# Sums of 40 rows turned round in a graph network's edge stage: features on partitions, W3 applied at once, counts from the activation, narrower tables, two banks

## The chip, the cores and the metric

The kernel runs on one core of a Trainium2 chip. The metric is the device time of one execution in microseconds (us). The data are one graph of 12,500 nodes with 48 features and 400,000 edges, all in fp32 on the path that matters here.

## The reference

Two layers, each fed with h = relu(layernorm(x)) and added to x. The edges are sorted by target (`dst`).

```python
def L0(x, src, dst, W, b):                    # first layer
    deg = bincount(src);  s = where(deg > 0, deg ** -0.5, 0)
    msg = (s[src] * s[dst])[:, None] * x[dst]
    return relu(segment_sum(msg, src, n) @ W.T + b)

def L1(x, src, dst, edge_attr, W1, b1, W2, b2, W3, b3):   # second layer
    edge = concatenate([x[src], x[dst], edge_attr], -1)   # 48 + 48 + 16 = 112
    h = relu(edge @ W1 + b1)                              # 128 features
    h = relu(h @ W2 + b2)                                 # 128 features
    message = h @ W3 + b3                                 # 48 features
    cnt = segment_sum(1, dst, n)
    return x + segment_sum(message, dst, n) / maximum(cnt, 1)[:, None]

h = relu(layernorm(x));  x = x + L0(h, src, dst, ...)
h = relu(layernorm(x));  x = x + L1(h, src, dst, edge_attr, ...)
```

The change touches the second layer's sums over the edges of a target, W3 and the counts. Since W3 is linear, both kernels sum h (128 features) over the edges of a target first and multiply the sums by W3; b3 enters times the count. The kernels also hold max(h@W2, -b2) instead of relu(h@W2 + b2), and add b2 back by way of `cb`, which is b2@W3 + b3, times the count.

## The kernel before

The stages ahead (to 2025.9 us) sort out the windows, count degrees, run the first layer, and leave in DRAM `htab`, the 48 features of every node, and `btab`, the part of W1 that belongs to the target, applied to every node (`x[dst] @ W1[48:96]`, 128 wide). With the zeros of `zero` the two tables `utab` of sums are cleared near the start, by 14 DMAs on SP's queue (helper `clear`).

The edge stage ("e1") goes over 782 chunks of 4 x 128 = 512 edges (the last chunk is one tile of 128). Two chunks (`Q`) share a window: 40 neighbouring target rows (`W`), in which all their edges end. For each chunk there are five steps:

- `fetch`: ACT copies 16 edge features into the tile `et` (L997); POOL issues four gathers of 128 rows each from `htab` into it (the helper `gather`, L225); ACT makes from the targets the one-hot window `mv[64:104]`, 40 rows by 512 edges, with a Square and a Relu (helper `window_of`, L641 and L647): relu(1 - (target - row)^2). Every second chunk SP loads the 40 rows of `btab` under the weights of W1, into one of five tiles `wk` (L994).
- `turn`: four transposes on PE (L1009) and a copy by ACT (L1010) put the 64 features of the 512 edges into `mv[:64]`.
- `first`: one matmul of 104 rows, that is W1 on the features and the window's rows of `btab` through the one-hot (L1015), and ACT's Relu with b1 (L1019).
- `second`: four matmuls with h1 as weights, so that edges lie on partitions (L1026); DVE makes the one-hot `oh` of each edge's place in the window (L1031), writes 1.0 into the 129th column of h2 (L1039), and takes the maximum with -b2 (L1040).
- `summed`: four matmuls with `oh` as weights (40 columns) and h2 as moving side (129 columns) into `u_all`, which holds 40 rows (L1053). A window's eight matmuls accumulate. At the second chunk ACT takes the 40x129 sums out (L1062) and SP writes them into one of the two tables `utab` at the window's first row (L1063); windows in turn use one half and the other of `u_all`, and one table and the other.

fp32 matmuls run in two passes (the transposes in one), so the profile counts eight for four matmuls and two for `first`. In the loop, iteration c issues `fetch(c)`, then `summed(c-6)`, `second(c-4)`, `first(c-2)` and `turn(c)`, 782 + 6 iterations in all. The order on each engine is fixed by a scheduler when the kernel is compiled: on PE it is in each iteration the sums of c-6, h2 of c-4, h1 of c-2 and the transposes of c. The number of buffers limits how far an engine runs ahead: `et` has 8, `mv` 6, `h1`, `oh` and `h2` 4 each; in PSUM `et_ps`, `h1_ps` and `h2_ps` have 2 banks each and `u_all` and `m_ps` one each.

```python
u_all = ps.tile([W, 2, 256], FP, name="u_all", bufs=1)      # L1067: two halves of one bank
...
for step, late in ((summed, 6), (second, 4), (first, 2), (turn, 0)):
    if 0 <= c - late < NC1:
        step(run[c - late])
```

When all windows of a block of nodes are written, `finish` (a generator of which each iteration runs one step) loads that block of both tables (L1078), adds them (L1085), copies the counts out of column 128 (L1088), transposes the sums on PE (L1094), takes them out (L1097), applies W3 (L1101), adds the counts times `cb` (L1106, L1112) and hands over to `updated`, which divides by the counts, adds the residuals (L955 to L960) and stores. There are nine blocks: six of 14 x 128 nodes, then 8, 4 and 2 x 128.

Of the kernel before, what the change touches and what calls it, by code (L numbers as in the profile page):

```python
# [20 lines left out]
def kernel(  # L21
# [36 lines left out]
    nc = tc.nc  # L58
    N, F = x.shape
    E = src.shape[0]  # L60
    EF = edge_attr.shape[1]
    H = w2.shape[0]
# [3 lines left out]
    ROWS = NH * P  # L66
# [3 lines left out]
    TABLE = ROWS + P  # L70
    B = 4
    F1 = F + 1
    H1 = H + 1
    W = 40
    Q = 2
    NCH = NT // B
# [2 lines left out]
    NC1 = NCH + 1  # L79
# [23 lines left out]
    blocks, h0 = [], 0  # L103
# [102 lines left out]
    ltab = dram.tile([ND, RUN + P], FP, name="ltab")  # L206
    dltab = dram.tile([NS, ND, P], BF, name="dltab")
    acc1 = dram.tile([TABLE, F1], FP, name="acc1")
    utab = [dram.tile([ROWS, H1], FP, name=f"utab_{k}") for k in range(2)]
    ZH = 14  # L210

    def clear(tables, w, engines, pool):
# [138 lines left out]
    clear(utab, H1, (nc.sync, nc.sync), rp)  # L351


    w0_t = const.tile([F, F], FP, name="w0_t")
# [40 lines left out]
    k = 2  # L395
# [240 lines left out]
    def window_of(db, p0, c, to):  # L636


        a = c % VG * B * P
        n = B if c < NCH else TAIL  # L640
        nc.scalar.activation(  # L641
            to.rearrange("p (j i) -> p j i", j=n),
            db[p0 : p0 + W, a : a + n * P].rearrange("p (i j) -> p j i", j=n),
            AF.Square,
            bias=wid[p0 : p0 + W, c // Q : c // Q + 1],
        )
        nc.scalar.activation(to, to, AF.Relu, scale=-1.0, bias=unit[p0 : p0 + W])  # L647
        return n

    hview = htab.rearrange("(h p) f -> p h f", p=P)  # L650
# [318 lines left out]
    with tc.If(fast > 0) as branch:  # L969
        with tc.tile_pool(name="e1", bufs=3) as wp, tc.tile_pool(  # L970
# [9 lines left out]
            def fetch(c):  # L980
                n = B if c < NCH else TAIL
                if c % VG == 0:
                    group["db"] = targets(wp, 64, c)
                    v = min(VG, NCH - c)
                    ea = wp.tile([P, VG, B, EF], FP, name="ea", bufs=2)
                    nc.scalar.dma_start(ea[:, :v], ea_view[:, c : c + v])
                    group["ea"] = ea
                db, ea = group["db"], group["ea"]
                if c == NCH:
                    nc.scalar.dma_start(ea[:, c % VG, 0, :], edge_attr[E4:])  # L990
                if c % Q == 0:
# [10 lines left out]
                window_of(db, 64, c, mv[64:, : n * P])  # L1002
                return dict(c=c, n=n, at=at, wc=wc, et=et, mv=mv)

            def turn(k):
# [16 lines left out]
            def second(k):  # L1022
                n, h1 = k["n"], k["h1"]
                h2_ps = ps.tile([P, B, H], FP, name="h2_ps")
                for j in range(n):
                    nc.tensor.matmul(  # L1026
                        h2_ps[:, j, :], h1[:, j * P : (j + 1) * P], w2_sb, start=True, stop=True
                    )
                c = k["c"]
                oh = wp.tile([P, B, W], FP, name="oh", bufs=4)  # L1030
                nc.vector.tensor_tensor(  # L1031
                    oh[:, :n],
                    rel[:, c * B : c * B + n].unsqueeze(2).to_broadcast([P, n, W]),
                    iota_f[:, None, :W].to_broadcast([P, n, W]),
                    OP.is_equal,
                )
                k["oh"] = oh
                h2 = wp.tile([P, B, H1], FP, name="h2", bufs=4)
                nc.vector.memset(h2[:, :, H:], 1.0)  # L1039
                nc.vector.tensor_tensor(  # L1040
                    h2[:, :n, :H],
                    h2_ps[:, :n],
                    b2_neg[:, None, :].to_broadcast([P, n, H]),
                    OP.max,
                )
                k["h2"] = h2

            def summed(k):
                n, oh, h2 = k["n"], k["oh"], k["h2"]
                q = k["c"] % Q  # L1050
                u_ps = u_all[:, k["c"] // Q % 2, :H1]
                for j in range(n):
                    nc.tensor.matmul(  # L1053
                        u_ps,
                        oh[:, j, :],
                        h2[:, j, :],
                        start=(q == 0 and j == 0),
                        stop=(q == Q - 1 and j == n - 1),
                    )
                if q == Q - 1:  # L1060
                    u = wp.tile([W, H1], FP, name="u", bufs=4)
                    nc.scalar.activation(u, u_ps, AF.Copy)  # L1062
                    nc.sync.dma_start(utab[k["c"] // Q % 2][bass.ds(k["at"], W), :], u)  # L1063

            u_all = ps.tile([W, 2, 256], FP, name="u_all", bufs=1)
            cb_ps = ps.tile([P, B, H], FP, name="m_ps", bufs=1)
            nc.tensor.matmul(  # L1067
                cb_ps[:, 0, :F], b2_col.to_broadcast([H, P]), w3_sb, start=True, stop=True
            )
            cb = wp.tile([P, F], FP, name="cb", bufs=1)  # L1070
            nc.vector.tensor_tensor(cb, cb_ps[:, 0, :F], b3_sb, OP.add)
            HB = blocks[0][1]

            def finish(h0, n):

                us = [wp.tile([P, HB, H1], FP, name=f"uk{k}", bufs=1) for k in range(2)]
# [10 lines left out]
                cnt = wp.tile([P, HB], FP, name="cnt", bufs=1)  # L1087
                nc.vector.tensor_copy(cnt[:, :n], us[0][:, :n, H])  # L1088
                upd = wp.tile([P, HB, F], FP, name="upd", bufs=1)
                for a in range(0, n, B):  # L1090
                    k = min(B, n - a)
                    m_ps = ps.tile([P, B, H], FP, name="m_ps", bufs=1)
                    for j in range(k):
                        nc.tensor.transpose(m_ps[:, j, :], us[0][:, a + j, :H], ident)  # L1094
                    yield
                    u_t = wp.tile([H, B, P], FP, name="u_t", bufs=1)
                    nc.scalar.activation(u_t[:, :k], m_ps[:, :k], AF.Copy)  # L1097
                    yield
                    m_ps = ps.tile([P, B, H], FP, name="m_ps", bufs=1)
                    for j in range(k):  # L1100
                        nc.tensor.matmul(  # L1101
                            m_ps[:, j, :F], u_t[:, j, :], w3_sb, start=True, stop=True
                        )
                    yield
                    cw = wp.tile([P, B, F], FP, name="cw", bufs=1)
                    nc.vector.tensor_tensor(  # L1106
                        cw[:, :k],
                        cnt[:, a : a + k].unsqueeze(2).to_broadcast([P, k, F]),
                        cb[:, None, :].to_broadcast([P, k, F]),
                        OP.mult,  # L1110
                    )
                    nc.vector.tensor_tensor(  # L1112
                        upd[:, a : a + k, :], m_ps[:, :k, :F], cw[:, :k], OP.add
                    )
                    yield
                updated(wp, h0, n, cnt[:, :n], upd[:, :n])

            def go_on():
                if ends and next(ends[0], "end") == "end":
# [1 line left out]

            coming, ends = list(blocks), []
            group, run = {}, []
            for c in range(NC1 + 6):
                run.append(fetch(c) if c < NC1 else None)
                for step, late in ((summed, 6), (second, 4), (first, 2), (turn, 0)):
                    if 0 <= c - late < NC1:
                        step(run[c - late])
                done = c + 1 - 6
                while coming and done >= coming[0][2]:  # L1130
                    h0, n, _ = coming.pop(0)
                    ends.append(finish(h0, n))
                go_on()
# [71 lines left out]
```

## Time and profile before

| | |
|---|---|
| Median of three runs | 6740.73 us (6739.53 to 6771.3) |
| The profiled execution, its own time | 6743.89 us |
| Its span (first to last instruction) | 6742.1 us |
| Mean granted clock of TensorE | 0.860 |
| First gather of the edge stage | 2025.9 us |
| Busy share of the span, PE / ACT / DVE / POOL | 68 / 58 / 38 / 46% |

The profile page lists one execution. In its slices, each column is a fortieth of the span (168.6 us) and a digit the busy share in tenths; the granted clock is in tenths of full speed. In its groups, a row is line, engine, operation, tiles (out <- in), shapes and count, then busy us in all and the mean ns of one, then the idle time of the engine just before these instructions and what ended most of it. In the waits, a row is who waited, for which row's end, us in total, times and the longest. "remote" is an end of a wait which the profile cannot lay to a row; "issue" is time in which the engine waited for nothing that is seen. In the timeline, a row is start us, duration us, engine, line, operation, shapes and count, and in brackets the idle time ahead of it. Releasers are inferred from the order in time, so an engine that finished just before is sometimes named where another had been the cause.

### The profile page before, as it was taken

To read this page: it belongs to the slowest core of one execution; us is meant where nothing else is said; L and a number is where in the kernel's file an instruction comes from. 1 tells how busy PE (TensorE), PEld (TensorE's weight loads), DVE (VectorE), ACT (ScalarE), POOL (GpSimd) and SP (SyncE) were. 2 spreads that over 40 slices of the span, in tenths; PEclk is the share of its full clock that TensorE was granted. 3 is DMA by queue.
4 is the path that set the end of the run, shared out by engine and by line. 5 is a ranking of instruction groups with operands and counts; after the bars stand their busy time and mean duration, and the time that the engine had idled before them with its cause. 6 is when DMAs were issued, how large, how long until landed. Compare 5 with 4: busy or idle time off the path is not lost. (4 is left out here: it accounts for less than half of the span.)

```text
span 6742.1 us, 97110 instructions
## 1 busy us (share of the span) xinstructions
PE 4613.8 (68%) x35368; PEld 3546.1 (53%) x35368; DVE 2539.2 (38%) x4116; ACT 3879.8 (58%) x7051; POOL 3080.8 (46%) x3239
## 2 busy tenths in 40 slices
PE   0400589999994776776777677777676777677777
PEld 0300489999993444544455455445454454445545
DVE  2995799999981111111111111111111111111112
ACT  1600178888884555655556555555555555555555
POOL 0003200000006666666666666666666666666664
PEclk9999699999996888888888888878888887888888
DMA  3001154444432222222222222222222222222221
GB/s 129 14 0 28 35 158 147 148 148 147 145 123 47 40 41 39 52 41 41 39 52 41 41 39 52 40 41 40 53 43 38 41 50 43 39 41 50 43 45 30
DMA packets 397378, 407.60 MB, mean 60 GB/s; under 512 B 227689, under 2 KB 351229, under 8 KB 392382
## 3 DMA queue, kind: packets, MB, share of 16 engines
q1 hardware_dynamic: 168166, 280.50, 14.8%
q0 software_dynamic: 103488, 85.03, 8.5%
q10 hardware_dynamic: 125238, 35.77, 2.3%
q8 instruction: 283, 4.64, 0.3%
q14 instruction: 203, 1.66, 0.1%
HBM read 363.00 MB, written 38.02 MB: 59 GB/s over the span
## 5 line engine op out<-in xcount | busy, mean ns | idle before, releaser
L225 POOL DMA_INDIRECT et<-htab,src_i x3125 | 2964.5, 949 | 3004.1 <-PE m_ps L1067 1300.9
L1053 PE MATMUL u_all<-h,oh 128*40 128x129 f32 x6250 | 1022.4, 314 | 1106.3 <-ACT u L1062 662.3
L1053 PEld LDWEIGHTS u_all<-h,oh 128*40 128x40 f32 x6250 | 739.1, 132 | 1358.3 <-ACT u L1062 773.1
L1019 ACT ACTIVATE h<-h_ps,b_sb 128x512 f32<-128x512 f32 x782 | 534.3, 683 | 1388.5 <-remote 701.4
L1040 DVE TENSOR_TENSOR h<-h_ps,b_neg 128x512 f32<-128x512 f32 x782 | 538.5, 689 | 1765.8 <-PE et_ps L1009 547.9
L1026 PE MATMUL h_ps<-w_sb,h 128*128 128x128 f32 x6250 | 1128.4, 332 | 75.1 <-issue 56.5
L1026 PEld LDWEIGHTS h_ps<-w_sb,h 128*128 128x128 f32 x6250 | 947.9, 231 | 267.2 <-issue 237.1
L842 ACT ACTIVATE rows<-at_ps 128x432 bf16<-128x432 f32 x1830 | 951.2, 531 | 147.9 <-DVE g L801 35.2
L1031 DVE TENSOR_TENSOR oh<-rel,iota_f 128x160 f32<-128x160 f32 x782 | 253.5, 324 | 2063.4 <-remote 679.5
L854 PE MATMUL sum<-rows,ohs 128*128 128x144 bf16 x10976 | 1008.5, 228 | 20.6 <-ACT rows L842 17.4
L1015 PE MATMUL h_ps<-mv,wk 104*128 104x512 f32 x1564 | 936.1, 681 | 28.5 <-issue 28.1
L641 ACT ACTIVATE mv<-db,wid 40x512 f32<-40x512 int32 x782 | 943.2, 1206 | 17.4
L854 PEld LDWEIGHTS <-ohs 128*128 128x128 bf16 x10976 | 855.4, 144 | 26.0 <-issue 19.8
L826 DVE TENSOR_TENSOR ohs<-lo_b,iota_x 128x4096 bf16<-128x4096 bf16 (+1 forms) x350 | 786.1, 2247 | 51.3 <-PE sum L854 33.0
L1009 PEld LDWEIGHTS et_ps<-ident,et 128*64 128x64 f32 x3125 | 365.8, 118 | 727.0 <-issue 618.4
L838 PE MATMUL at_ps<-g,oht 112*128 112x144 bf16 x5488 | 651.1, 226 | 36.0 <-DVE oht L822 35.6
L1009 PE MATMUL et_ps<-ident,et 128*64 128x128 f32 x3125 | 541.6, 286 | 172.1 <-issue 132.1
L647 ACT ACTIVATE mv<-mv,unit 40x512 f32<-40x512 f32 x782 | 560.1, 716 | 19.9
L1010 ACT ACTIVATE mv<-et_ps 64x512 f32<-64x512 f32 x782 | 453.4, 580 | 202.1 <-remote 102.1
L838 PEld LDWEIGHTS <-oht 112*128 112x128 bf16 x5488 | 416.1, 98 | 39.0 <-issue 36.0
L1015 PEld LDWEIGHTS h_ps<-mv,wk 104*128 104x128 f32 x1564 | 286.4, 226 | 43.6 <-issue 43.5
L1062 ACT ACTIVATE u<-u_all 40x129 f32<-40x129 f32 x391 | 106.0, 271 | 316.5 <-remote 215.6
(202 smaller groups left out, 2193.3 us busy)
## 6 DMA issues: line engine op xcount, KB each, us to landing
at<-dltab SPq DMA_DIRECT2D x343, 448.0 KB
db<-in_dst_dram SPq DMA_DIRECT2D x97, 640.0 KB
et<-htab,src_i POOLq DMA_INDIRECT x3125
ea<-in_edge_attr_dram ACTq DMA_DIRECT2D x97, 256.0 KB
utab<-zero SPq DMA_DIRECT2D x14, 903.0 KB
uk<-utab SPq DMA_DIRECT2D x12, 903.0 KB
utab<-u SPq DMA_DIRECT2D x391, 20.2 KB
wk<-btab SPq DMA_DIRECT2D x391, 20.0 KB
```

What stands on the lines that cost most here:

```text
L225: nc.gpsimd.indirect_dma_start(out=into, out_offset=None, in_=table, in_offset=bass.IndirectOffsetOnAxis(ap=idx, axis=0),)
L641: nc.scalar.activation(to.rearrange("p (j i) -> p j i", j=n), db[p0 : p0 + W, a : a + n * P].rearrange("p (i j) -> p j i", j=n), AF.Square ...
L647: nc.scalar.activation(to, to, AF.Relu, scale=-1.0, bias=unit[p0 : p0 + W])
L826: nc.vector.tensor_tensor(ohs[:, :n], lo_b[:, h0 : h0 + n, None, c : c + CG].to_broadcast([P, n, S, CG]), iota_x[:, None].to_broadcast([P, ...
L838: nc.tensor.matmul(ps3[:, i, :], oht[:, k, c % CG, :], g3[:, c, :], start=True, stop=True)
L842: nc.scalar.activation(rows[:, : len(tiles)], ps3[:, : len(tiles)], AF.Copy)
L854: nc.tensor.matmul(sums[k][:, j, :], ohs[:, k, j * P : (j + 1) * P, c % CG], rows[:, i, :], start=(c == 0 and j == 0), stop=(c == ND - 1 a ...
L1009: nc.tensor.transpose(et_ps[:, j * P : (j + 1) * P], et[:, j, :], ident)
L1015: nc.tensor.matmul(h1_ps[:, : n * P], k["wc"], k["mv"][:, : n * P], start=True, stop=True)
L1026: nc.tensor.matmul(h2_ps[:, j, :], h1[:, j * P : (j + 1) * P], w2_sb, start=True, stop=True)
L1040: nc.vector.tensor_tensor(h2[:, :n, :H], h2_ps[:, :n], b2_neg[:, None, :].to_broadcast([P, n, H]), OP.max,)
L1053: nc.tensor.matmul(u_ps, oh[:, j, :], h2[:, j, :], start=(q == 0 and j == 0), stop=(q == Q - 1 and j == n - 1),)
```

## The change

- `summed`: h2 is now the weights and `oh` the moving side, so that the sums come out with 128 features on partitions and 40 rows as columns. They have their own PSUM tile `u_ps`, a whole bank, two of them in turn. ACT takes the 128x40 sums out at the second chunk (L1065, tile `u_t`). In h2 the column of ones goes, and its memset.
- `applied`, a new step eight iterations after `fetch`: one matmul with `u_t` as weights applies W3 (L1072) and writes 40x48 into another part of the same bank (columns 256 to 303, partitions 64 to 103); ACT takes it out (L1074), DVE adds the counts of the two chunks as the 49th column (L1075), SP writes 40x49 into the table (L1078).
- The counts come from the sum that ACT's Relu in `window_of` now writes out (`accum_out`), one number per row of the window and chunk, in the tile `cnt_w`.
- The tables have 49 columns instead of 129, and so have their clears and the loads of `finish`, which loses the transposes, their evictions, W3 and the copy of the counts.
- The loop runs 782 + 8 iterations, and a block is finished two iterations later.

```diff
-    utab = [dram.tile([ROWS, H1], FP, name=f"utab_{k}") for k in range(2)]
+    utab = [dram.tile([ROWS, F1], FP, name=f"utab_{k}") for k in range(2)]
...
-        nc.scalar.activation(to, to, AF.Relu, scale=-1.0, bias=unit[p0 : p0 + W])
+        nc.scalar.activation(
+            to, to, AF.Relu, scale=-1.0, bias=unit[p0 : p0 + W], accum_out=count
+        )
...
-                h2 = wp.tile([P, B, H1], FP, name="h2", bufs=4)
-                nc.vector.memset(h2[:, :, H:], 1.0)
+                h2 = wp.tile([P, B, H], FP, name="h2", bufs=4)
...
             def summed(k):
                 n, oh, h2 = k["n"], k["oh"], k["h2"]
                 q = k["c"] % Q
-                u_ps = u_all[:, k["c"] // Q % 2, :H1]
+                if q == 0:
+                    group["u_ps"] = ps.tile([H, 512], FP, name="u_ps")
+                k["u_ps"] = group["u_ps"]
+                u_ps = k["u_ps"][:, :W]
                 for j in range(n):
                     nc.tensor.matmul(
                         u_ps,
+                        h2[:, j, :],
                         oh[:, j, :],
-                        h2[:, j, :],
                         start=(q == 0 and j == 0),
                         stop=(q == Q - 1 and j == n - 1),
                     )
                 if q == Q - 1:
-                    u = wp.tile([W, H1], FP, name="u", bufs=4)
-                    nc.scalar.activation(u, u_ps, AF.Copy)
-                    nc.sync.dma_start(utab[k["c"] // Q % 2][bass.ds(k["at"], W), :], u)
-
-            u_all = ps.tile([W, 2, 256], FP, name="u_all", bufs=1)
...
+                    u_t = wp.tile([H, W], FP, name="u_t", bufs=3)
+                    nc.scalar.activation(u_t, u_ps, AF.Copy)
+                    k["u_t"] = u_t
+
+            def applied(k):
+                c = k["c"]
+                if c % Q == Q - 1:
+                    m_ps = k["u_ps"][64:K1, 256 : 256 + F]
+                    nc.tensor.matmul(m_ps, k["u_t"], w3_sb, start=True, stop=True)
+                    u = wp.tile([P, F1], FP, name="u", bufs=4)
+                    nc.scalar.activation(u[64:K1, :F], m_ps, AF.Copy)
+                    nc.vector.tensor_tensor(
+                        u[64:K1, F:], cnt_w[64:K1, c - 1 : c], cnt_w[64:K1, c : c + 1], OP.add
+                    )
+                    nc.sync.dma_start(utab[c // Q % 2][bass.ds(k["at"], W), :], u[64:K1, :])
...
             def finish(h0, n):
...
-                for a in range(0, n, B):
-                    z = slice(a, min(a + B, n))
-                    nc.vector.tensor_tensor(us[0][:, z], us[0][:, z], us[1][:, z], OP.add)
-                    yield
...
-                        nc.tensor.transpose(m_ps[:, j, :], us[0][:, a + j, :H], ident)
...
-                            m_ps[:, j, :F], u_t[:, j, :], w3_sb, start=True, stop=True
...
+                u, cnt = us[0][:, :n, :F], us[0][:, :n, F]
+                nc.vector.tensor_tensor(us[0][:, :n], us[0][:, :n], us[1][:, :n], OP.add)
+                yield
+                cw = wp.tile([P, HB, F], FP, name="cw", bufs=1)
...
+                nc.vector.tensor_tensor(cw[:, :n], cw[:, :n], u, OP.add)
...
-            for c in range(NC1 + 6):
+            for c in range(NC1 + 8):
                 run.append(fetch(c) if c < NC1 else None)
-                for step, late in ((summed, 6), (second, 4), (first, 2), (turn, 0)):
+                for step, late in (
+                    (applied, 8), (summed, 6), (second, 4), (first, 2), (turn, 0)
+                ):
...
-                done = c + 1 - 6
+                done = c + 1 - 8
```

In the compiled order of after, PE's work of an iteration is no longer in four clean pieces: transposes stand between the sums, h2 and h1, and L1072 of one window stands between the sums of the next window's two chunks. ACT's L998 (the former L997) stands two chunks ahead of the transposes instead of seven, and L640 (the former L641) one instead of three to four. POOL's order is as before.

More of the change, by code (lines that the diff above doesn't have):

```diff
@@ L72 @@
     F1 = F + 1
-    H1 = H + 1
     W = 40
@@ L349 @@
             nc.scalar.activation(ov[:, c], tp.rearrange("p b q -> p q b"), AF.Copy)
-    clear(utab, H1, (nc.sync, nc.sync), rp)
+    clear(utab, F1, (nc.sync, nc.sync), rp)
     w0_t = const.tile([F, F], FP, name="w0_t")
@@ L634, in window_at, with window_of @@
         return nc.sync.value_load(db[p0 : p0 + 1, a : a + 1], min_val=0, max_val=N - 1)
-    def window_of(db, p0, c, to):
+    def window_of(db, p0, c, to, count):
         a = c % VG * B * P
@@ L1001, in fetch @@
                 mv = wp.tile([K1, B * P], FP, name="mv", bufs=6)
-                window_of(db, 64, c, mv[64:, : n * P])
+                window_of(db, 64, c, mv[64:, : n * P], cnt_w[64:K1, c : c + 1])
                 return dict(c=c, n=n, at=at, wc=wc, et=et, mv=mv)
@@ L1037, in second @@
                 k["oh"] = oh
-                h2 = wp.tile([P, B, H1], FP, name="h2", bufs=4)
-                nc.vector.memset(h2[:, :, H:], 1.0)
+                h2 = wp.tile([P, B, H], FP, name="h2", bufs=4)
                 nc.vector.tensor_tensor(
-                    h2[:, :n, :H],
+                    h2[:, :n],
                     h2_ps[:, :n],
@@ L1060, in summed @@
                 if q == Q - 1:
-                    u = wp.tile([W, H1], FP, name="u", bufs=4)
-                    nc.scalar.activation(u, u_ps, AF.Copy)
-                    nc.sync.dma_start(utab[k["c"] // Q % 2][bass.ds(k["at"], W), :], u)
-            u_all = ps.tile([W, 2, 256], FP, name="u_all", bufs=1)
[L1066 to L1069, printed above, removed]
+                    u_t = wp.tile([H, W], FP, name="u_t", bufs=3)
[12 more added lines that the diff above has]
+                    nc.sync.dma_start(utab[c // Q % 2][bass.ds(k["at"], W), :], u[64:K1, :])
+            cnt_w = wp.tile([P, NC1], FP, name="cnt_w", bufs=1)
+            cb_ps = ps.tile([H, 512], FP, name="u_ps")[:, :F]
+            nc.tensor.matmul(cb_ps, b2_col.to_broadcast([H, P]), w3_sb, start=True, stop=True)
             cb = wp.tile([P, F], FP, name="cb", bufs=1)
-            nc.vector.tensor_tensor(cb, cb_ps[:, 0, :F], b3_sb, OP.add)
+            nc.vector.tensor_tensor(cb, cb_ps, b3_sb, OP.add)
             HB = blocks[0][1]
             def finish(h0, n):
-                us = [wp.tile([P, HB, H1], FP, name=f"uk{k}", bufs=1) for k in range(2)]
+                us = [wp.tile([P, HB, F1], FP, name=f"uk{k}", bufs=1) for k in range(2)]
                 for k in range(2):
@@ L1082, in finish @@
                 yield
-                for a in range(0, n, B):
-                    z = slice(a, min(a + B, n))
-                    nc.vector.tensor_tensor(us[0][:, z], us[0][:, z], us[1][:, z], OP.add)
-                    yield
[L1087 to L1093, printed above, removed]
-                        nc.tensor.transpose(m_ps[:, j, :], us[0][:, a + j, :H], ident)
[L1095 to L1101, printed above, removed]
-                            m_ps[:, j, :F], u_t[:, j, :], w3_sb, start=True, stop=True
[L1103 to L1115, printed above, removed]
@@ L1116, in finish @@
-                updated(wp, h0, n, cnt[:, :n], upd[:, :n])
+                u, cnt = us[0][:, :n, :F], us[0][:, :n, F]
+                nc.vector.tensor_tensor(us[0][:, :n], us[0][:, :n], us[1][:, :n], OP.add)
+                yield
+                cw = wp.tile([P, HB, F], FP, name="cw", bufs=1)
+                nc.vector.tensor_tensor(
+                    cw[:, :n],
+                    cnt.unsqueeze(2).to_broadcast([P, n, F]),
+                    cb[:, None, :].to_broadcast([P, n, F]),
+                    OP.mult,
+                )
@@ L1118, in go_on @@
+                yield
+                nc.vector.tensor_tensor(cw[:, :n], cw[:, :n], u, OP.add)
+                yield
+                updated(wp, h0, n, cnt, cw[:, :n])
             def go_on():
```

## The prediction

> **What bounds the kernel now.** The profiled execution took 6743.89 us, 3.2 us over the median of 6740.73 us of the three runs; its span is 6742.1 us. All sums below are made in this span, and 3 us are taken off at the end. I read the slices first, then the groups, the waits and the timeline.
>
> The slices, POOL's row and the granted clock (each column is 168.6 us):
>
> ```profile
> POOL 0003200000006666666666666666666666666664
> PEclk9999699999996888888888888878888887888888
> ```
>
> From the 13th slice on POOL works without change: it is the edge stage, which runs from the first gather at 2025.9 us to 6742.1 us, 4716 us or 70% of the span. Nearly all that the change touches is here. 782 chunks in 4667 us (2025.9 to the last gather at 6692.7) are 5.97 us a chunk. The groups give the two ends of this:
>
> ```profile
> L225 POOL DMA_INDIRECT et<-htab,src_i x3125 | 2964.5, 949 | 3004.1 <-PE m_ps L1067 1300.9
> L1053 PE MATMUL u_all<-h,oh 128*40 128x129 f32 x6250 | 1022.4, 314 | 1106.3 <-ACT u L1062 662.3
> L1019 ACT ACTIVATE h<-h_ps,b_sb 128x512 f32<-128x512 f32 x782 | 534.3, 683 | 1388.5 <-remote 701.4
> ```
>
> A gather is 0.95 us busy and, back to back, starts 1.25 us after the one before (timeline below). So four gathers are 5.0 us a chunk: POOL's floor for the stage is 3125 x 1.25 = 3906 us. The 750 us between 3906 and 4667 us are pauses of POOL. PE waits 1106 us at one place, the first matmul of the sums (L1053). The waits from 2100 to 6700 us:
>
> ```profile
> PEld u_all L1053 <- ACT u L1062: 773.1, 185, 12.8
> ACT h L1019 <- remote: 692.2, 105, 28.1
> PE u_all L1053 <- ACT u L1062: 662.3, 172, 7.6
> POOL et L225 <- ACT h L1019: 439.7, 143, 4.0
> ACT u L1062 <- remote: 215.6, 55, 7.9
> ```
>
> (PEld and PE are the same wait seen twice.) PE waits for ACT's eviction L1062, since both halves of `u_all` are one tile in one bank; ACT itself waits "remote". The timeline shows what that means:
>
> ```profile
> 3190.39 0.91 PE L1009 MATMUL et_ps<-ident,et 128*64 128x128 f32 x4
> ...
> 3192.59 0.94 POOL L225 DMA_INDIRECT et<-htab,src_i  x1 [0.30 <-issue]
> 3193.07 0.69 DVE L1040 TENSOR_TENSOR h<-h_ps,b_neg 128x512 f32<-128x512 f32 x1 [6.06 <-remote]
> 3195.16 0.69 ACT L1019 ACTIVATE h<-h_ps,b_sb 128x512 f32<-128x512 f32 x1 [6.74 <-remote]
> ...
> 3196.68 0.94 POOL L225 DMA_INDIRECT et<-htab,src_i  x1 [3.15 <-ACT mv L1010]
> ...
> 3197.81 0.27 ACT L1062 ACTIVATE u<-u_all 40x129 f32<-40x129 f32 x1
> ...
> 3198.14 1.94 PE L1053 MATMUL u_all<-h,oh 128*40 128x129 f32 x8 [6.83 <-ACT u L1062]
> ```
>
> PE has done its transposes by about 3191.3 us and stands for 6.83 us. ACT is idle for 6.74 us of that, though the matmuls that L1019 reads had ended at 3190.6; it goes on only when POOL's row of twelve gathers (from 3178.8, the last at 3192.59) has ended. Most such rows (202 of 291) are of exactly twelve, three chunks, then POOL pauses 2.9 us: 15 + 2.9 = 17.9 us for three chunks, the 5.97 us. So POOL runs until it has no buffer, the others learn late of what PE has done, and PE stands at L1053. When the gathers are over (after 6693 us) there is no such wait, and from one L1053 row to the next are 3.39 us (6709.05 to 6712.44).
>
> **The change part by part.**
>
> *The sums.* h2 becomes the weights (128 columns) and the one-hot rows the moving side (40 instead of 129 columns); eight matmul passes a chunk as before. The nearest rows stand side by side near the end, at full clock:
>
> ```profile
> 6724.54 0.99 PE L1101 MATMUL m_ps<-w_sb,u_t 128*128 128x48 f32 x8
> 6725.46 1.08 PE L1053 MATMUL u_all<-h,oh 128*40 128x129 f32 x8
> 6726.47 1.16 PE L1026 MATMUL h_ps<-w_sb,h 128*128 128x128 f32 x8
> ```
>
> Eight passes of the old form take 6726.47 - 6725.46 = 1.01 us; eight with 128 weight columns and 48 moving ones 0.92 us. So the new form is worth between 0 and 0.09 x 782 = -70 us; I take 0, as PE has 1106 us of waits here.
>
> The Trainium skill speaks against this part: "TensorE: Matmul & The Clock Gate", step-by-step section, says that the time of a weight load goes by its columns, with columns / 1.2 ns: an estimate of 107 ns against 33. By this page, if the load were bare, 6250 passes would cost 458 us more. The rows above differ: 128 columns and 40 go at one pace, and the measurement decides.
>
> *W3 at once.* 391 times two passes (L1072): 782 x 0.115 (the L1101 row) = +90 us of PE. The finish loses 98 transposes and 98 matmuls of two passes: 294 x 0.12 = -35 us. Net +55 us at full clock, up to +110 at half; I charge 30, because PE has waits to hide most of it, and keep 0 to 110. The compiled order puts L1072 of a group between the sums of the next group's two chunks; there it waits for the eviction L1065, issued an iteration before. If this eviction is as late as ACT's in the timeline, then all that PE has queued behind it (sums, h2, h1, transposes, hence POOL's buffers) is late with it; that is part of rival D.
>
> *Two banks.* In before the first sum of a group waits for L1062 of the group just finished, about half an iteration earlier in PE's order. In after it waits for L1074 of the group two back, and L1072 for L1065: one to one and a half iterations. So PE gains about one chunk of lead; a wait of 6.8 us is not longer than that lead plus an iteration at half clock (6.2 to 7 us in the trace). What is late next is the pair of banks of `et_ps` and `h1_ps`, whose lead is two iterations, and POOL's buffers.
>
> *ACT.* The Relu of the window gets an accumulator read. The row for it, and its pace:
>
> ```profile
> 94.45 0.23 ACT L364 ACTIVATE spare<-xt 128x48 f32<-128x48 f32 x1
> 94.58 0.19 ACT L364 ACTIVATION_READ_ACCUMULATOR spare<-xt 128x1 f32 x1
> 94.68 0.23 ACT L364 ACTIVATE spare<-xt 128x48 f32<-128x48 f32 x1
> ```
>
> It adds 0.10 (by pace) to 0.19 us. Per pair, one eviction of 0.27 (L1062) gives way to two, 0.25 (L1065, by L997's 0.256) and 0.23 (L1074, by L364): +0.21, or 0.105 a chunk. So +0.205 to +0.295 us a chunk on 3.58 us (L641 1.21, L647 0.72, L1019 0.68, L1010 0.58, L997 0.26, half of 0.27): +160 to +231 us of ACT. As long as the period is 5.97 us a chunk, ACT has over 2 us of idle time in it and the cost is 0; if ACT's idle time cannot be used, all of it counts (rival D). L641 and L998 also come later in ACT's order than before (one and two chunks ahead of the transposes instead of three and seven), which takes cover from ACT.
>
> *DVE.* 782 memsets of 0.06 us go, 391 additions of one column come (about 0.16 us, the L955 row): nothing, DVE is busy 806 of 4600 us. DVE's and PE's extra semaphore steps (about 1870 and 360) are not seen as rows; PE's pauses "issue" at a change of groups are 0.19 to 0.32 us, so 360 of them are at most +115 us and at least 0; I take 0.
>
> *Tables.* 49 columns instead of 129: writes of 7.7 KB for 20.2, clears of 343 KB for 903. The writes are on SP, off the chain. The clears lie at 75 to 173 us on SP's queue, where DVE waits 51.5 us for transposed indices that are loaded beside them: 0 to -10, I take -3. At the end L1094 to L1112 go from the last block (6734.8 to 6737.4, some 2.6 us) and two evictions with a matmul come: -1.
>
> **Sum of the likeliest case (B).** PE's extra chunk of lead lets one more chunk through each time, so that rows of twelve gathers become sixteen: 20 + 2.9 = 22.9 us for four chunks, 5.72 a chunk. 782 x (5.97 - 5.72) = -195. Then 6743.9 - 195 + 30 - 3 - 1 = 6575, less 3: **6570 us**. With two more chunks (27.9 / 5 = 5.58) it is about -305, 6440 without PE's 30; with half of the gain 6670. That is B's own range. Chance 0.45.
>
> **The rivals.**
>
> A. *POOL becomes the bound.* If the wait at L1053 alone made the signals late, all pauses go: 2025.9 + 3906 + 49 (tail after the last gather) = 5981; with up to a third of the 750 us left, 6230. For it: PE's largest wait goes, and 5.0 us is all that four gathers need. Against it: DVE and ACT wait "remote" for h1 and h2 too (692 us and more), and these links stay. Chance 0.13.
>
> C. *No change.* The wait at L1053 is a shadow: POOL's row of gathers keeps the signals back, PE would stand at the next matmul that reads ACT's work, and POOL's pause stays. 6710 to 6770. For it: ACT resumes as POOL's row ends, whatever PE waits for. Chance 0.12.
>
> D. *Slower: ACT sets the pace of the awake part.* In the 17.9 us for three chunks ACT and DVE are awake some ten, and in them ACT does 3 x 3.58 = 10.7 us of work (some of it ahead). If the asleep part is fixed by POOL, every 0.1 us that ACT gains per chunk lengthens the period: +160 to +231, plus 0 to 55 for PE's matmuls, less 3: 6900 to 7030, middle 6965. It decides once ACT's added work is not met by a shorter sleep, that is if L1019's "remote" total stays near 690 us. For it: evictions and Relus stand in one ACT order, and the window's work moves nearer to its use. Against it: ACT is busy 2687 of 4600 us, and PE's lead grows. Chance 0.30.
>
> That the second bank is not used, so that nothing is gained, is in C; the compiled waits speak against it.
>
> **How the numbers follow.** Faster by over 0.5% (about what this measurement can tell from no change): A and B, 0.58. Within: C, 0.12. Slower: D, 0.30. The range leaves out A (0.13) and the top of D (0.07): 6250 to 6980.
>
> **What would show it.** B: rows of 16 or more gathers; the wait of PE at the first sum well under 1106 us; POOL's pauses 500 to 560 us. A: POOL's pauses under 250 us. C: the wait reappears at L1009 or L1015 with the same rows of twelve. D: "remote" at L1019 unchanged, ACT busier by 160 us or more, PE waiting at L1072 or for the window's rows. The pace of L1053's successor over 0.13 us at full clock would show that 128 weight columns do cost. A mistake in the cause of the late signals, which I have only seen to go with POOL's rows of gathers, would make all four sums wrong.

## The result, and the profile after

The changed kernel took 6927.32 us (median of 6 runs, 6915.75 to 6953.42), the kernel before 6753.42 us beside it (6 runs, 6732.59 to 6773.08): a ratio of 1.0262, 95% interval 1.0230 to 1.0295. It is slower by 174 us, where 6570 us had been forecast. The profiled execution has a span of 6928.5 us. The page's slices of after, POOL's row and the granted clock:

```profile
POOL 0004100000006666666656566666666666666664
PEclk9999599999996777777877777777777777777777
```

POOL's digit is the same 6 with some 5s, and the clock fell from 8 to 7: from 2100 to 6700 us its mean is 0.76, where before had 0.82. The stage of the edges, first to last gather, takes 4821 us (2055.9 to 6877.2) instead of 4667. It also begins 30 us later, but that is scatter: in the kernels below that are made from before, it began at 2046.7 (b_banks), 2058.7 (b_acc) and 2037.4 (b_pause2k), and at 2017.6 to 2025.7 in the others.

The groups of after that answer to those shown of before, and behind them before's rows of the same two matmuls, h1 and the transposes:

```profile
L224 POOL DMA_INDIRECT et<-htab,src_i x3125 | 2973.8, 952 | 3181.6 <-PE u_ps L1082 1333.2
L1016 PE MATMUL h_ps<-mv,wk 104*128 104x512 f32 x1564 | 1140.0, 818 | 723.9 <-ACT mv L1011 528.4
L1011 ACT ACTIVATE mv<-et_ps 64x512 f32<-64x512 f32 x782 | 460.8, 589 | 1644.0 <-remote 1006.7
...
L1056 PE MATMUL u_ps<-oh,h 128*128 128x40 f32 x6250 | 1083.7, 323 | 84.0 <-ACT u L1074 43.0
...
L1010 PE MATMUL et_ps<-ident,et 128*64 128x128 f32 x3125 | 814.8, 321 | 252.7 <-ACT et L998 186.9
```

```profile
L1015 PE MATMUL h_ps<-mv,wk 104*128 104x512 f32 x1564 | 936.1, 681 | 28.5 <-issue 28.1
...
L1009 PE MATMUL et_ps<-ident,et 128*64 128x128 f32 x3125 | 541.6, 286 | 172.1 <-issue 132.1
```

PE's wait at the sums has gone, as the two banks promise: 84 us at L1056, where L1053 had 1106. But h1's matmul (L1016) now waits 724 us, where before has 28.5 us at its L1015, and the transposes (L1010) wait 253 us instead of 172, most of it for ACT's L998. In the waits the same pair shows on both sides:

```profile
ACT mv L1011 <- remote: 1002.5, 188, 13.3
...
POOL et L224 <- ACT mv L1011: 857.3, 325, 4.5
...
PE h_ps L1016 <- ACT mv L1011: 527.7, 203, 7.4
```

ACT waits for the transposes (L1011 is their copy into `mv`), and PE, having nothing else in front, stands at the very next matmul until that copy is done. The timeline of after shows one such wait:

```profile
3198.03 0.38 PE L1010 MATMUL et_ps<-ident,et 128*64 128x128 f32 x2
...
3199.03 0.27 PE L1010 MATMUL et_ps<-ident,et 128*64 128x128 f32 x1
3199.14 0.39 PE L1027 MATMUL h_ps<-w_sb,h 128*128 128x128 f32 x2
...
3203.96 0.59 ACT L1011 ACTIVATE mv<-et_ps 64x512 f32<-64x512 f32 x1 [6.04 <-remote]
...
3204.60 1.22 PE L1016 MATMUL h_ps<-mv,wk 104*128 104x512 f32 x1 [5.08 <-ACT mv L1011]
```

Counted through from the first chunk, the first of the two transposes in the row at 3198.03 is the last of its chunk and ends at 3198.3. Three transposes of the next chunk (the last ends at 3199.3) and four h2 matmuls follow, to 3199.5, and then h1 of the first chunk is due. ACT takes up the copy 5.7 us after the chunk's transposes have ended, and PE loses 5.08 us.

The compiled order tells why. In before, 21 matmuls stand between a chunk's last transpose and its h1 (a few more where a block is finished beside it). In after the numbers are 0, 8, 12, 7, 8, 18, 14 and 9 in turn, over eight chunks. For chunks 400 and 401 (T transposes, U sums, G h2, H h1, A the window's W3):

```
before  T400*4 U395*4 G397*4 H399 T401*4 U396*4 G398*4 H400
after   T400*4 H400 U396 T401 U396*3 A395 U397 T401 U397*3 G399 T401 G399*2 T401 G399 G400 T402 ...
```

### The profile page after: what moved, and what is told of

It is laid out like the page before. It is cut to its first block, busy times and chain, and to the rows that moved or that the text cites. A ratio compares the mean times of both kernels' runs of the same rounds, so it can differ in the third digit from the quotient of the medians.

```text
span 6928.5 us, 101116 instructions
## 1 busy us (share of the span) xinstructions
PE 4933.8 (71%) x35856; PEld 3966.7 (57%) x35856; DVE 2586.1 (37%) x3659; ACT 4033.7 (58%) x8196; POOL 3083.0 (44%) x3239
## 4 chain that ended last, share of the span: by engine, by line
PE 32%; another core or an unknown queue 15%; ACT 13%; issue 5%; DMA 2%; POOL 0%; SPq 0%; ACTq 0%; DVE 0%; POOLq 0%; DVEq 0%
PE u_ps L1056 10%; PE h_ps L1027 9%; PE h_ps L1016 8%; ACT mv L640 6%; PE et_ps L1010 4%; ACT mv L646 2%; ACT mv L1011 2%; ACT h L1020 2%; DMA ea<-in_edge_attr_dram 1%; DMA et<-htab,src_i 1%; PE u_ps L1072 1%; ACT et L998 1%; ACT u L1074 0%; POOL et L224 0%
## 5 line engine op out<-in xcount | busy, mean ns | idle before, releaser
L1016 PE MATMUL h_ps<-mv,wk 104*128 104x512 f32 x1564 | 1140.0, 818 | 723.9 <-ACT mv L1011 528.4
L1011 ACT ACTIVATE mv<-et_ps 64x512 f32<-64x512 f32 x782 | 460.8, 589 | 1644.0 <-remote 1006.7
L1027 PE MATMUL h_ps<-w_sb,h 128*128 128x128 f32 x6250 | 1282.6, 344 | 161.7 <-issue 142.4
L1027 PEld LDWEIGHTS h_ps<-w_sb,h 128*128 128x128 f32 x6250 | 1146.2, 253 | 371.1 <-issue 254.3
L1040 DVE TENSOR_TENSOR h<-h_ps,b_neg 128x512 f32<-128x512 f32 x782 | 533.3, 689 | 2051.7 <-remote 961.2
L1056 PEld LDWEIGHTS u_ps<-oh,h 128*128 128x128 f32 x6250 | 1022.7, 242 | 316.4 <-ACT u L1074 163.7
L1056 PE MATMUL u_ps<-oh,h 128*128 128x40 f32 x6250 | 1083.7, 323 | 84.0 <-ACT u L1074 43.0
L1010 PE MATMUL et_ps<-ident,et 128*64 128x128 f32 x3125 | 814.8, 321 | 252.7 <-ACT et L998 186.9
L640 ACT ACTIVATE mv<-db,wid 40x512 f32<-40x512 int32 x782 | 943.9, 1207 | 19.2
L1016 PEld LDWEIGHTS h_ps<-mv,wk 104*128 104x128 f32 x1564 | 314.4, 248 | 814.7 <-ACT mv L1011 586.8
L1010 PEld LDWEIGHTS et_ps<-ident,et 128*64 128x64 f32 x3125 | 434.9, 143 | 548.3 <-ACT et L998 241.1
L823 DVE TENSOR_SCALAR oht<-at,index 112x2048 bf16<-112x2048 bf16 (+1 forms) x350 | 258.0, 737 | 0.7 <-PE at_ps L839 0.7
```

The source lines that it names most:

```text
L640: nc.scalar.activation(to.rearrange("p (j i) -> p j i", j=n), db[p0 : p0 + W, a : a + n * P].rearrange("p (i j) -> p j i", j=n), AF.Square ...
L1010: nc.tensor.transpose(et_ps[:, j * P : (j + 1) * P], et[:, j, :], ident)
L1016: nc.tensor.matmul(h1_ps[:, : n * P], k["wc"], k["mv"][:, : n * P], start=True, stop=True)
L1027: nc.tensor.matmul(h2_ps[:, j, :], h1[:, j * P : (j + 1) * P], w2_sb, start=True, stop=True)
L1056: nc.tensor.matmul(u_ps, h2[:, j, :], oh[:, j, :], start=(q == 0 and j == 0), stop=(q == Q - 1 and j == n - 1),)
```

## The experiments

The theory that these views suggest, called **order**: the scheduler's new order of PE's instructions puts h1 close behind its own transposes, so each late signal reaches PE sooner. Its rivals: **ACT**, which was rival D of the forecast (the accumulator read and the second eviction set the pace), and for the missing gain **PE's lead** (case B) against **rows** (POOL's unbroken gathers keep the signals late, whatever PE's lead, which is case C at its root). Every ratio is to the kernel before on the same chip, with its 95% interval. "Late" counts the chunks, of 781, whose maximum on DVE (L1040 of before and its like) starts over 3 us after the last h2 matmul has ended; before has 439, after 273. It is a rough measure, since earlier work on DVE and full buffers also hold the maximum up: in 214 of before's 439, DVE had stood idle for over 3 us just ahead of it. (Some expectations have up to four more, counted a little differently.)

### Order, ACT, and two banks alone (one chip, before 6797.78)

**a_peorder.** Each PE instruction of the edge stage is pinned behind the one written before it:

```diff
-                    nc.tensor.transpose(et_ps[:, j * P : (j + 1) * P], et[:, j, :], ident)
+                    tc.keep_in_program_order(
+                        nc.tensor.transpose(et_ps[:, j * P : (j + 1) * P], et[:, j, :], ident)
+                    )
...  (and so for h1, h2, the sums and W3)
```

> The kernel after with its PE instructions of the edge stage kept in the written order (W3 of the window, sums, h2, h1, transposes, each in one piece), nothing else changed. Theory 'order' (PE's interleaved order put h1 straight behind the transposes of its own chunk, so that PE waits for ACT's copy L1011): PE's wait at h1 falls from 528 us to under 150 and the time to 6600-6780. Theory 'ACT' (rival D: the accumulator read and the second eviction on ACT set the pace): time stays at 6870-6960, with PE waiting elsewhere for ACT.

Measured: 6838.19, ratio 1.0045 (1.0023 to 1.0066). Most of the loss of 1.0262 is gone, though the kernel does exactly the same work. h1's wait in its page:

```profile
L1018 PE MATMUL h_ps<-mv,wk 104*128 104x512 f32 x1564 | 1100.3, 790 | 84.5 <-issue 75.6
...
L1011 PE MATMUL et_ps<-ident,et 128*64 128x128 f32 x3125 | 607.1, 321 | 429.9 <-ACT et L998 306.8
```

From 724 to 84.5 us. The upper end of "order" (6780) was missed by 58 us in time; in the ratio, which leaves out that this chip's before is 44 us slower than the one beside after, little is left. What is left stands at the transposes, which wait for ACT's L998.

**a_bothorder.** ACT's order too: `fetch` seven chunks ahead, the window three ahead, ACT's instructions pinned, and six weight tiles `wk` instead of five.

```diff
+                    (applied, 8), (summed, 6), (windowed, -3), (second, 4), (first, 2), (turn, 0)
```

> As a_peorder, and ACT's order of the edge stage fixed too: edge features seven chunks ahead, the window's Square and Relu three ahead, as in the kernel before (one more weight tile wk, six instead of five). Theory 'order': the waits of the transposes for L998 (184 us) go as well, 6500-6740. Theory 'ACT': the work is the same, 6870-6960.

Measured: 6795.88, ratio 0.9985 (0.9966 to 1.0003), 56 us above the range of "order", of which 44 us are this chip's. The transposes' wait falls from 430 to 122 us:

```profile
L1017 PE MATMUL et_ps<-ident,et 128*64 128x128 f32 x3125 | 618.0, 325 | 122.2 <-issue 105.3
```

The changed kernel is level with before. So both orders together account for the whole slow-down, ACT's (with the sixth weight tile, which was not tried alone) for 42 us of it on this chip. "ACT" fails: the work is unchanged. So does the clock as a cause: its mean from 2100 to 6700 us is 0.74 here, lower than in after.

**b_acc.** Before with the accumulator output alone:

```diff
-        nc.scalar.activation(to, to, AF.Relu, scale=-1.0, bias=unit[p0 : p0 + W])
+        nc.scalar.activation(
+            to, to, AF.Relu, scale=-1.0, bias=unit[p0 : p0 + W], accum_out=count
+        )
```

> The kernel before with the accumulator output of the window's Relu added, 782 accumulator reads (nobody reads the counts; the column of ones stays). Theory 'ACT': 782 x 0.10 to 0.19 us = +78 to +149, 6820-6890. Theory 'order': ACT's added work lies in its idle time, 6710-6780.

Measured: 6800.15, ratio 0.9994 (0.9976 to 1.0012). The reads cost nothing here; "ACT" fails again.

**b_banks.** Before with the sums in two banks:

```diff
-                u_ps = u_all[:, k["c"] // Q % 2, :H1]
+                if q == 0:
+                    group["u_ps"] = ps.tile([P, B, H], FP, name="u_ps")
+                u_ps = group["u_ps"][:W].rearrange("w b h -> w (b h)")[:, :H1]
```

> The kernel before with the sums in two PSUM tiles of a bank each (the finish takes its PSUM from the same two), nothing else. The forecast's case B (one chunk more of lead for PE): PE's wait at the sums falls from 1106 us to under 600, time 6440-6670. Case C (the wait is the shadow of late signals): the wait moves to the next matmul that reads ACT's work and the time stays at 6705-6785. Theory 'order' says nothing against B.

Measured: 6786.40, ratio 0.9968 (0.9950 to 0.9986): 0.3% instead of the 2.5% of case B. From its waits:

```profile
DVE h L1040 <- remote: 774.1, 93, 78.2
ACT h L1019 <- remote: 713.2, 109, 12.1
...
POOL et L225 <- ACT h L1019: 619.1, 186, 4.3
...
PE u_ps L1055 <- DVE h L1040: 374.1, 166, 23.5
```

PE no longer waits for the eviction, but it waits for DVE's h2 instead. ACT's Relu waits "remote" as long as in before (713 us against 692) and DVE's maximum longer (774 against 516). Rows of exactly twelve gathers are at least as common as in before (221 of 278), and 489 chunks are late. This is case C: the wait at the sums was a shadow.

### h1 straight behind its transposes (before 6738.01)

**b_hbehind.** The reverse test, in the kernel before, with PE pinned:

```diff
-                for step, late in ((summed, 6), (second, 4), (first, 2), (turn, 0)):
+                for step, late in ((summed, 6), (second, 4), (turn, 0), (first, 0)):
```

> The kernel before with h1's matmul of a chunk straight behind that chunk's four transposes on PE (0 matmuls between, where before has 21), the other pieces in the written order. Theory 'order': PE waits there for ACT's copy of the transposes in every chunk, at least 0.6 to 1 us awake and longer when signals are late: 6900-7300. If the order of PE's pieces is not what made the kernel after slower: 6750-6850.

Measured: 6991.48, ratio 1.0377 (1.0360 to 1.0394). Its page:

```profile
L1017 PE MATMUL h_ps<-mv,wk 104*128 104x512 f32 x1564 | 1096.2, 789 | 1476.9 <-ACT mv L1012 1283.3
```

The same wait as in after, twice as long: 684 of the 782 chunks now have no matmul between. Part of it is the copy itself (0.59 us): half of the copies start within 0.5 us of the last transpose, and only 189 chunks are late. Nothing else of the change is in this kernel. Its clock, 0.888 over the span, is above before's.

### What keeps the signals late

**b_half and a_both_half** (before 6793.05). Half of the gathers are left out of before, and of a_bothorder:

```diff
-                for j in range(n):
+                for j in range(0, n, 2):
                     t = c * B + j
                     gather(et[:, j, :F], htab, src_i[:, t : t + 1])
...
-                    nc.tensor.transpose(et_ps[:, j * P : (j + 1) * P], et[:, j, :], ident)
+                    nc.tensor.transpose(et_ps[:, j * P : (j + 1) * P], et[:, j - j % 2, :], ident)
```

> The kernel before with two of a chunk's four gathers left out; the transposes of the other two tiles read the same rows, so half of the edges have another edge's source features. POOL needs 2.5 us a chunk. 'Rows': rows of gathers are short (two to six), and a chunk takes PE's 3.4 us or ACT's 3.6 us and a little: 4700-5300. 'PE's lead': PE's wait for ACT at the sums stays at about 1.5 us a chunk: 5500-6500.

> The same two gathers left out of the kernel after with PE's and ACT's orders fixed (a_bothorder). If the change's own work (accumulator read, second eviction, W3 at once) costs anything where POOL does not bound, it shows here against b_half: ACT's +0.2 to 0.3 us a chunk, +160 to +230; if the second bank is worth something there, -100 or more; the 'order' theory gives within 60 us of b_half.

Measured: 4862.15, ratio 0.7162 (0.7136 to 0.7187), and 4932.14, ratio 0.7250 (0.7230 to 0.7270). With two gathers a chunk, a chunk of before takes 3.56 us (4805.2 - 2024.0 over 781), 3 chunks are late instead of 439, and PE hardly waits at all. The windows from 2100 to 4700 us (us, then busy us of PE, PEld, DVE, ACT, POOL, the clock):

```profile
2100.00:4700.00 2600.00, 2526.52 (x16330) 1818.81 (x16331) 796.38 (x2301) 2525.92 (x4044) 1384.39 (x1462) 1.00 0.27 58
```

ACT is busy 97% and the clock is full. Here, where PE and ACT bound, the changed kernel's own work shows: +70 us, 0.09 us a chunk (67 us from the first to the last gather of the two profiled executions); "order" had put at most 60, "ACT" 160 to 230. The gathers that are left out take their DMA traffic with them, so this test does not part POOL's issuing from the traffic.

**b_pause8, b_pause2k** (same chip), **b_pause512, b_pause1k, a_pause512** (before 6738.01), **b_pause768, a_pause1k** (before 6792.76). POOL gets a memset after each chunk's gathers, of a tile that nobody reads, 8 to 2048 columns wide; all but b_pause8 have PE's written order pinned, which leaves before's order on PE as it was (21 matmuls, in the traces of both kinds):

```diff
                     tc.keep_in_program_order(gather(et[:, j, :F], htab, src_i[:, t : t + 1]))
+                tc.keep_in_program_order(nc.gpsimd.memset(pad, 0.0))
```

> The kernel before with one tiny memset by POOL (128x8) after each chunk's four gathers, nobody reads it. Theory 'rows' (what PE has done reaches ACT, DVE and POOL late as long as POOL issues gathers without a break; this, not PE's lead, sets 17.9 us for three chunks): if any other instruction on POOL is a break, the late stretches go, and POOL's own pace decides, 5.0 us plus 0.1 to 0.6 a chunk: 6000-6450. If a break must be POOL standing idle for some us: 6720-6850, rows go on. Theory 'PE's lead' (case B, longer rows with more lead): no effect, 6700-6800.

> As b_pause8 with a memset of 128x2048 on POOL, some 2 us, after each chunk's gathers, and PE's instructions kept in the written order (the order of the kernel before). 'Rows': POOL takes 5.0 + about 2 us a chunk, 7 us, so 7500, unless the break leaves ACT and DVE awake; the lags of ACT behind PE should be under 2 us in most chunks. 'PE's lead': lags as before, about 7 us in two chunks of three.

> The kernel before (PE's written order fixed) with a POOL memset of 128x512, about 0.5 us, after each chunk's four gathers. 'Rows': if 0.5 us without a gather is break enough, the late stretches go and POOL sets 5.0 + 0.4 us a chunk: 6250-6350. If the break is too short: as b_pause8, no change, 6760-6840.

> As b_pause1k with a memset of 128x768, about 0.75 us: POOL's own pace is 5.0 + 0.6 us a chunk. 'Rows': if this break is long enough in most chunks, 6480-6580; if the late chunks come back as with 128x512 (385 of 782 over 3 us late on DVE, against 63 with 128x1024), 6600-6690, and no length of memset does better than about 6600.

> The same with 128x1024, about 0.95 us. 'Rows': 5.0 + 0.8 us a chunk if the break is enough: 6600-6680 with lags of ACT behind PE under 1 us as in b_pause2k; if not, 6760-6900.

| memset | its us | late of 781 | time | ratio to before (interval) |
|---|---|---|---|---|
| 128x8 | 0.12 | 419 | 6798.09 | 1.0009 (0.9994 to 1.0025) |
| 128x512 | 0.54 | 381 | 6703.95 | 0.9949 (0.9932 to 0.9965) |
| 128x768 | 0.76 | 424 | 6739.24 | 0.9925 (0.9900 to 0.9951) |
| 128x1024 | 0.97 | 60 | 6627.47 | 0.9845 (0.9823 to 0.9867) |
| 128x2048 | 1.82 | 0 | 7290.90 | 1.0723 (1.0693 to 1.0754) |

Work that slows POOL makes the kernel faster, up to a point: with 0.97 us between groups of four gathers nearly all signals are in time. b_pause1k came in the range that "rows" gave (6600 to 6680), and b_pause2k has no late chunk, as it said. b_pause8 refutes that any instruction on POOL is break enough (6000 to 6450); b_pause512 fell between its two ranges and b_pause768 above both. With 0.97 us PE waits for the gathered rows that it needs and for hardly anything else, as b_pause1k's waits show:

```profile
DVE oh L1036 <- PE u_all L1058: 1659.8, 479, 9.7
PEld et_ps L1013 <- DMA et<-htab,src_i: 1423.2, 1099, 6.4
PE et_ps L1013 <- DMA et<-htab,src_i: 1097.2, 752, 6.2
ACT mv L1015 <- PE et_ps L1013: 894.6, 435, 7.3
```

No "remote" is left among the first. With 1.82 us POOL is the bound at 6.69 us a chunk. b_pause1k beats both kernels: 1.6% under before.

> The kernel after with PE's and ACT's orders fixed (a_bothorder) and the 128x512 memset on POOL after each chunk's gathers. As b_pause512 within 40 us: where POOL sets the pace the change's own work is hidden.

> The kernel after with PE's and ACT's orders fixed and the 128x1024 memset on POOL after each chunk's gathers. If the change has any gain left once the signals come in time, it is below b_pause1k's 0.9845 of before by more than 0.5%; if POOL's pace hides both, 0.980-0.990.

With the changed kernel in its fixed order, the memsets of 512 and 1024 columns gave 6714.46, ratio 0.9965 (0.9951 to 0.9979), and 6723.66, ratio 0.9903 (0.9881 to 0.9926), with 423 and 515 chunks late. The change shows no gain of its own. With 1024 columns it is still late where before is not, at the same pace of the gathers; the cause was not found. These two ran on different chips, and the changed kernel's clock was lower (0.73 against 0.87 from 2100 to 6600 us).

**b_each320** (before 6792.76): the memset, 128x320 wide (0.38 us), stands after every single gather.

> A memset of 128x320 (about 0.35 us) after every single gather instead of one long one after four: the same pace of POOL as b_pause1k, about 5.85 us a chunk, but no long break. If an unbroken break of about a us is what lets the signals through: late as with 128x128 or 128x512, 6800 or more. If the mean pace of gathers is what counts: as b_pause1k, 6600-6680.

Measured: 6752.50, ratio 0.9940 (0.9918 to 0.9962). The gathers start 1.50 us apart, and only 10 chunks are late. So no long break is needed; a slower mean pace does it. The time lies between the two expectations because the memset made POOL slower than planned (5.99 us a chunk, not 5.85), and POOL is then the bound. b_pause768, at 1.40 us a gather in the mean where POOL does not wait, was late; b_pause1k, at 1.46, nearly not.

**b_each224, b_each224_again, a_each320.** A memset of 224 columns after every gather, to find a faster pace in time; and b_each320's in a_bothorder.

> A memset of 128x224 (about 0.28 us) after every gather: a pitch of about 1.41 us, 5.65 us a chunk. If the pace of 1.50 us (b_each320: 10 chunks over 3 us late on DVE) can be raised this far without late signals: 6440-6520. If 1.41 is too fast again (b_pause768, 1.40 us in the mean: 427 late): 6650-6760.

> The kernel after with PE's and ACT's orders fixed and the 128x320 memset after every gather (pitch 1.50 us). If the pace of the gathers alone decides: fewer than 50 chunks late and 0.994 of before like b_each320. If the kernel after is late at a pace at which before is not (a_pause1k: 519 chunks late, b_pause1k: 63): over 200 late and 1.00 or more of before.

> The same kernel as b_each224, which met a chip on which the kernel before itself took 5960 us, with no late signal in the trace. If this chip is like the others (before at 6740-6800): a pitch of 1.41 us in time gives 6490-6520; late again as with b_pause768 gives 6650-6760. If before takes 5960 here too: 6497 again.

Measured: 6496.91, 6749.98 and 6497.13. But on the two chips that ran these, the kernel before itself took 5959.52 us (7 runs, 5956.82 to 5962.26) and 5962.23 us (7 runs, 5960.90 to 5963.43): 12% less than on the others, with nothing changed. The ratios, 1.0904 (1.0886 to 1.0922), 1.1328 (1.1309 to 1.1347) and 1.0896 (1.0878 to 1.0914), say that there the memsets only cost POOL time: 3125 x 1.414 us is 4419, and from the first to the last gather b_each224 takes 4449 us. In the traces of all three no chunk is late; in b_each224's, PE's waits for ACT are gone:

```profile
DVE oh L1035 <- PE u_all L1057: 2635.8, 746, 10.3
PEld et_ps L1012 <- DMA et<-htab,src_i: 1337.6, 1031, 6.3
ACT mv L1014 <- PE et_ps L1012: 1073.0, 494, 7.3
```

At 1.50 us a gather the slower chip (b_each320, 6752.50) and the quick one (a_each320, 6749.98) take the same time, since POOL bounds both.

No trace of before itself on a quick chip was kept, but 5960 us is rival A's figure (5981): POOL's floor of 3906 us for the gathers, with no pause. The old kernel reached it, so by its time late signals cost it nothing there, and lateness at a gather pitch of 1.25 us belongs to some chips (or to a state that they are in) and not to the kernel alone. The records of semaphore updates (the counts by which one engine learns of another's work) part the two kinds of chip as well: from the first to the last gather, b_each224's trace has 5503 updates of PE's semaphore for 5503 instructions that make one, and 3719 of ACT's for 3720; before's trace, on a slower chip, has 4618 for 5458 and 1886 for 3701, though ahead of the stage it has 2899 of PE's 2909. These are records that are missing, since the engines go on, and they are missing in b_half too (1951 of PE's 3138), where hardly a chunk is late.

Since these three ran on quick chips only, they do not tell whether a slower chip is in time at 1.41 us. For those it is known no closer than that 1.40 us is too fast and 1.46 to 1.50 us mostly slow enough, for before; the changed kernel at 1.46 us was late. The changed kernel's ratio without memsets on a quick chip was not measured.

## Why the prediction was wrong

- **"PE's extra chunk of lead lets one more chunk through each time"** is the step that failed. It took PE's 1106 us at L1053 for a cause. b_banks has that lead and nothing else of the change: the wait moved to DVE's h2, rows of twelve stayed, and 0.3% came of 2.5%. The -195 us term should have been about -20 us (by the ratio; the two medians differ by 11). Nor did rows of sixteen come with the whole change: in after 130 of 406 rows are of twelve, and most others are shorter.
- **C was right about the two banks**, and given 0.12. Its argument, that ACT resumes as POOL's row of gathers ends whatever PE waits for, is what b_half and the memsets show on the slower chips: thin out the gathers, and the signals are in time.
- **D had the sign and the size** (6900 to 7030, measured 6927) by luck, for a wrong reason. Its own sign is missing: ACT's "remote" wait at the h1 Relu fell from 692 to 81 us. ACT's added work was priced well: the accumulator read takes 0.18 us, L1065 0.204 and L1074 0.206 where 0.25 and 0.23 were put. But it costs nothing where ACT has idle time (b_acc 0.9994). With ACT bound, the whole change costs 70 us (a_both_half against b_half), under D's 160 to 231.
- **The term that was missing is PE's compiled order.** It was known: the section on the change names it. I priced L1072's place in it, but put nothing for how close h1 stands behind its own transposes, 0 to 18 matmuls instead of 21; PE waits 724 us there instead of 28.5. Of a moved step every wait counts, and here it was one that the diff doesn't touch. a_peorder takes 1.0262 to 1.0045 with that alone, and b_hbehind, in the other direction, makes 1.0377 out of before.
- **ACT's order was seen and put under "takes cover from ACT"** without a price. It is 42 us: the transposes' 430 us of waiting for L998 in a_peorder against 122 in a_bothorder.
- **128 weight columns are not slower**, as the rows had said. At full clock near the end of after:

```profile
6909.68 0.98 PE L1056 MATMUL u_ps<-oh,h 128*128 128x40 f32 x8
...
6910.59 0.28 PE L1072 MATMUL u_ps<-w_sb,u_t 128*40 128x48 f32 x2
...
6910.80 0.86 PE L1056 MATMUL u_ps<-oh,h 128*128 128x40 f32 x6
```

  Eight passes take 6910.59 - 6909.68 = 0.91 us against 1.01 of the old form; this is the 0 to -70 us that was bounded, and L1072's two take 0.21 where 0.23 was put. The rule of the Trainium skill ("TensorE: Matmul & The Clock Gate", step-by-step section) that a load goes by its columns shows in part in the load rows near the two ends: 116 ns for L1053's 40 columns and 192 for L1056's 128 (medians; the prediction had 33 and 107 by the page), but also 111 for the transposes' 64. It does not show in the pace, since the loads lie beside other passes.

What stays open: by what way gathers at 1.25 us hold up what others learn of PE, and why on some chips only. The runs show that it goes with the pace of POOL's gathers, in before most clearly (a_pause1k is the exception), and that it comes with both layouts of the sums. Before's trace narrows it: what is late is the update of PE's semaphore, and not the engine that waits for it. In the prediction's timeline ACT's L1019 starts at 3195.16, 0.02 us after such an update, though its matmuls had ended at 3190.6. Over its 202 rows of twelve gathers, 333 updates are recorded 8 to 16 us after a row's first gather, where 2143 of the instructions that make them end (PE's ends are modelled); then 2279 come in 2 us. What holds the updates up was not found. I also don't know which part of the change made the scheduler interleave: with two banks alone or the accumulator alone it does not.

## What to carry to other kernels

When a scheduler writes the order, compare for each consumer how many instructions stand between it and its producer on the engine that will wait, before and after, and price a shrunken distance like a new wait; pinning the old order is then the first experiment. A large wait that names one releaser may be the shadow of something common to all: try the remedy alone, and thin out the suspected engine, before crediting the whole wait to a change. And measure the unchanged kernel on the same chip each time, since here it moved by 12% between chips.

## What the runs showed of the hardware that was not expected

- The kernel before took 5960 us on two chips and 6738 to 6798 us on the others used, with narrow scatter on each.
- On the slower ones, while POOL issues gathers every 1.25 us, ACT and DVE act late on PE's results; in before, 439 of 781 chunks are over 3 us late on DVE, and a tenth 8.6 us or more. In its rows of twelve gathers, of what PE ends for them in the first 6 us about a fifth is taken up over 3 us late, and from 8 us on nearly all. The first of that is taken up 3.2 us (median) after the row's last gather has started, when the late updates of PE's semaphore come. At 1.50 us a gather, 10 chunks are late.
- On a slower chip, 0.97 us of useless work on POOL per chunk made the kernel before 1.6% faster, with 60 chunks late.
